# Two store queues, a moved bias add and an earlier transpose in a conditional-residual kernel

## The chip, the cores and the metric

The kernel runs on one core of one Trainium2 chip. The metric is the device time of one launch in microseconds; the span of a profile is the part of it in which the core's engines and queues execute the program.

## What is computed

The input x has 128 batches of 128 tokens and 512 channels. Each batch has a language number, and each of the ten language numbers names a set of weights and rows.

```
w1, w2 = W1[language_ids], W2[language_ids]          # 512x128 and 128x512
h = relu(x @ w1 + b1[language_ids])
y = x + h @ w2 + b2[language_ids]
mean, var = y.mean(-1), ((y - mean) ** 2).mean(-1)
out = x + (y - mean) * rsqrt(var + 1e-5) * gamma[language_ids] + beta[language_ids]
```

All of it is in float32.

## The kernel before, in words

A batch is one tile of 128 partitions (its tokens) by 512 channels. The batches go through a pipeline of stages, and each batch uses all engines:

- TensorE (PE) transposes x in four blocks (`transpose_x`, line 234), multiplies with w1 in four blocks (`down`, line 257) and with w2 (`up`, line 274, two matmul rows in the profile). For a few batches `up` starts with one more matmul that adds b2 into the same accumulator (line 273). Which ones is decided by `b2_by_matmul`.
- ScalarE (ACT) copies the transposed x out of PSUM (line 238), applies b1 and relu (`relu`, line 265), copies w1 of the batch from a resident table (`stage_w1`, line 225) and squares y for the variance (line 310; 394 for the last batches).
- GpSimd (POOL) adds b2 to x (`add_b2`, line 244; not for batches whose b2 comes from a matmul or from VectorE) and beta to x (`add_beta`, line 251). The second sum is the output tile o.
- VectorE (DVE) sums y with its row sums (`residual`, line 291), takes the negative means (line 298), refines the reciprocal root in three small steps (lines 324, 326, 329), scales with gamma (`scale`, line 353) and finishes o (line 362; `finish_cols`, line 419, for the last batches).
- SyncE's queue (SP) issues nearly all transfers. Stores carry two batches each (line 366); the last six batches are stored one by one (`store_last`, line 415).

The order on every engine is written out by hand: `keep` ties each instruction to the one before it on its engine, a DMA to the queue that issues it. A queue waits at an instruction whose inputs are missing, and what stands behind it waits too.

At the start PE runs empty matmuls (`spin`, line 477) while the first loads come. The 30 rows of beta, gamma and b2 are then spread over all partitions: DVE splits the rows into three bfloat16 parts (lines 183 to 187), PE multiplies each with a selecting column (`spread`, line 205) and ACT or DVE copies the result (lines 208 and 210). Between the rows PE does the first batches' transposes (`x_turn`) and down-projections.

At the end `tail` orders the last four batches, 124 to 127, and the ends of 122 and 123 (E is 123). Batches 123 and 124 are finished by ACT and POOL (`by_pool`: line 408 on ACT, 410 and 412 on POOL), 125 half by DVE and half by POOL, 126 and 127 by DVE.

Of the kernel before, what the change touches and what calls it, by code (L numbers as in the profile page):

```python
# [26 lines left out]
def cond_resid_kernel(ctx: ExitStack, tc: tile.TileContext, x, itok, W1, b1, W2, b2, gamma, beta, out):  # L27
# [8 lines left out]
    nc = tc.nc  # L36
    B, S, H = x.shape
# [8 lines left out]
    def keep(ins):  # L46

        engine = ins.ins.engine
        if engine in last:
            tc.add_manual_dep(ins.ins, last[engine], behind, reason="kept order")  # L50
        last[engine] = ins.ins.name
        return ins
# [14 lines left out]
    E = B - 5  # L67
# [6 lines left out]
    def xb(b):  # L74
        return xs[b // G][:, b % G, :]
# [57 lines left out]
    def lid(b, engine):  # L133
        g = b // G
        if (g, engine) not in lids:
            loads, vals = nc.values_load_multi_w_load_instructions(  # L136
                lang[0:1, g * G : (g + 1) * G],
                engines=[engine],
                min_val=0,
                max_val=L - 1,  # L140
                skip_runtime_bounds_check_because="clamped on the chip to 0..L-1 above",
            )
            for ins in loads:
                keep(ins)
            lids[g, engine] = vals
        return lids[g, engine][b % G]
# [65 lines left out]
    xT, hT, rs, os, ys, ssqs, nmeans, rstds = {}, {}, {}, {}, {}, {}, {}, {}  # L212
# [1 line left out]


    def b2_by_matmul(b):
        return b in (0, 1, 2, 3, 5) or (b % 32 == 30 and b < E)

    def b2_by_vector(b):
        return 8 <= b < B - 8 and (b % 4 == 1 if b < 24 else b % 16 in (1, 6, 11))  # L220
# [6 lines left out]
    def transpose_x(b):  # L227
        pxs[b] = p_x.tile([P, KC, P], FP, tag="xT", name=f"pxT_{b}")
        for k in range(KC):
            if b < EARLY:  # L230
                cols = xb(b).rearrange("s (p k) -> s k p", k=KC)[:, k, :]
            else:
                cols = xb(b)[:, k * P : (k + 1) * P]
            keep(nc.tensor.transpose(pxs[b][:, k, :], cols, ident))  # L234

    def copy_xT(b):
        xT[b] = tp.tile([P, KC, P], FP, tag="xT", name=f"xT_{b}")
        keep(nc.scalar.copy(xT[b], pxs.pop(b)))  # L238
# [38 lines left out]
    def col(tiles, b):  # L277

        return tiles[b // 2][:, b % 2 : b % 2 + 1]
# [6 lines left out]
    def residual(b):  # L286
        r = rs.pop(b) if b in rs else xb(b)
        if b % 2 == 0:
            sums[b // 2] = st.tile([P, 2], FP, tag="sum", name=f"sum_{b // 2}")
        keep(  # L290
            nc.vector.scalar_tensor_tensor(ys[b], ys[b], 1.0, r, ALU.mult, ALU.add, accum_out=col(sums, b))  # L291
        )

    def negative_means(g):

        nmeans[g] = st.tile([P, 2], FP, tag="nmean", name=f"nmean_{g}")
        keep(
            nc.vector.scalar_tensor_tensor(  # L298
                nmeans[g], sums[g], -1.0 / H, ys[2 * g + 1][:, 0:2], ALU.mult, ALU.bypass
            )  # L300
        )
# [20 lines left out]
    def newton(n, ssq, t, u):  # L322
        if n == 1:
            keep(nc.vector.scalar_tensor_tensor(u, ssq, EPS * H3, t, ALU.add, ALU.mult))  # L324
        else:
            keep(nc.vector.scalar_tensor_tensor(u, u, 1.0 / H3, t, ALU.mult, ALU.mult))

    def newton_3(rstd, t, u):
        keep(nc.vector.scalar_tensor_tensor(rstd, u, -3.0, t, ALU.add, ALU.mult))
# [11 lines left out]
    def rstd(g, n):  # L341
        t, u = of_pair(g)
        if n < 3:
            newton(n, ssqs[g], t, u)
        else:
            rstds[g] = st.tile([P, 2], FP, tag="rstd", name=f"rstd_{g}")
            newton_3(rstds[g], t, u)
            del ssqs[g], parts_of[g]

    def scale(b):  # L350
        v = lid(b, ET.DVE)
        keep(
            nc.vector.scalar_tensor_tensor(  # L353
                ys[b], ys[b], col(nmeans, b), gamma_b[:, bass.ds(v * H, H)], ALU.add, ALU.mult
            )
        )

    def finish(b):
        g, j = divmod(b, 2)
        o = os[g][:, j, :]  # L360
        keep(
            nc.vector.scalar_tensor_tensor(o, ys.pop(b), rstds[g][:, j : j + 1], o, ALU.mult, ALU.add)  # L362
        )

    def store(g):
        keep(nc.sync.dma_start(out=out[2 * g : 2 * g + 2].rearrange("b s h -> s b h"), in_=os.pop(g)))
        del rstds[g]
# [8 lines left out]
    def of_one(b):  # L376
        if -b not in parts_of:
            pool, tag = {E + 3: (p_h, "h"), E + 4: (p_x, "xT")}.get(b, (p_s, "s"))
            parts_of[-b] = pool.tile([P, 1], FP, tag=tag, name=f"root_of_{b}"), st.tile([P, 1], FP, tag="part", name=f"part_of_{b}")
        return parts_of[-b]  # L380

    def rstd_of(b, n):

        t, u = of_one(b)
        if n < 3:
            newton(n, ssqs[b], t, u)
        else:
            rstds[b] = st.tile([P, 1], FP, tag="rstd", name=f"rstd_{b}")
            newton_3(rstds[b], t, u)

    def deviation_of(b):
        ssqs[b] = st.tile([P, 1], FP, tag="ssq", name=f"ssq_{b}")
        sq = tp.tile([P, H], FP, tag="sq", name=f"sq_{b}")
        keep(nc.scalar.activation(sq, ys[b], AF.Square, bias=col(sums, b), scale=-float(H), accum_out=ssqs[b]))
        root(ssqs[b], of_one(b)[0])

    def rstd_col(b):
        return rstds[b] if b > E else rstds[b // 2][:, b % 2 : b % 2 + 1]
# [5 lines left out]
    def by_pool(b, scaled, cols=slice(0, H)):  # L404

        n = rp.tile([P, H], FP, tag="r", name=f"n_{b}")[:, cols]
        bias = 0.0 if scaled else shifts[b]
        keep(nc.scalar.activation(n, ys[b][:, cols], AF.Identity, bias=bias, scale=rstd_col(b)))
        if not scaled:
            keep(nc.gpsimd.tensor_tensor(n, n, gamma_b[:, bass.ds(lid(b, ET.Pool) * H, H)], ALU.mult))  # L410
        o = os[b // 2][:, b % 2, cols]
        keep(nc.gpsimd.tensor_tensor(o, n, o, ALU.add))  # L412

    def store_last(b):
        keep(nc.sync.dma_start(out=out[b], in_=os[b // 2][:, b % 2, :]))

    def finish_cols(b, cols=slice(0, H)):
        o = os[b // 2][:, b % 2, cols]
# [2 lines left out]
    def tail(b):  # L421
        p = E // 2
        residual(b)
        if b == E + 1:
            rstd(p, 1)
            scale(E - 1)
            rstd(p, 2)
            finish(E - 2)
            store(p - 1)
            rstd(p, 3)  # L430
            deviation_of(b)
            shift(E)
            by_pool(E, False)
        elif b == E + 2:
            rstd_of(b - 1, 1)
            negative_means(b // 2)
            rstd_of(b - 1, 2)
            finish_cols(E - 1)
            store_last(E - 1)
            rstd_of(b - 1, 3)  # L440
            store_last(E)
            deviation_of(b)
        elif b == E + 3:
            left, right = slice(0, H // 2), slice(H // 2, H)
            shift(b - 2)
            by_pool(b - 2, False)
            residual(b + 1)
            store_last(b - 2)
            rstd_of(b - 1, 1)
            scale(b - 1)  # L450
            rstd_of(b - 1, 2)
            negative_means(b // 2)
            deviation_of(b)
            scale(b)
            rstd_of(b - 1, 3)
            rstd_of(b, 1)
            deviation_of(b + 1)
            rstd_of(b, 2)
            finish_cols(b - 1, right)
            by_pool(b - 1, True, left)  # L460
            rstd_of(b, 3)
            scale(b + 1)
            rstd_of(b + 1, 1)
            finish_cols(b)
            store_last(b)
            rstd_of(b + 1, 2)
            store_last(b - 1)
            rstd_of(b + 1, 3)
            finish_cols(b + 1)
            store_last(b + 1)  # L470


    def spin(n, width):
        idle = p_s.tile([P, H], FP, tag="s", name="idle")
        for _ in range(n):
            keep(
                nc.tensor.matmul(
                    idle[:, :width], lhsT=ones, rhs=ones[:, 0:1].to_broadcast([P, width]), start=True, stop=True
                )
            )  # L480


    spin(11, H)

    def spread_turn(lo, hi):
        for r in range(lo, hi):
            spread(r, nc.scalar if r % 7 in (1, 3, 5) else nc.vector)

    def x_turn(b):
        transpose_x(b)  # L490
        copy_xT(b)

    spread_turn(0, 2)
    transpose_x(0)
    transpose_b1()
    copy_xT(0)
    spread_turn(2, 6)
    x_turn(1)
    spread_turn(6, 11)
    down(0)  # L500
    relu(0)
    spread_turn(11, 15)
# [14 lines left out]
    for i in range(3, B + U):  # L517
        b = i - U - 1
# [109 lines left out]
```

## Time and profile before

| | us |
|---|---|
| median of 3 runs (lowest to highest) | 310.78 (310.55 to 310.95) |
| the profiled execution | 310.83 |
| its span | 309.07 |
| last POOL instruction ends | 304.42 |
| last DVE instruction ends | 303.69 |

| engine | busy us | share of the span |
|---|---|---|
| PE | 295.1 | 95% |
| DVE | 294.8 | 95% |
| ACT | 280.4 | 91% |
| POOL | 285.5 | 92% |

Times in the profile count from the span's start. In a timeline a row has the start, the time taken, the engine (with a q for its queue's own instructions, such as issuing a DMA), the line, the operation and out<-in. In a list of waits a row has who waited, for whom, the sum in us, the number of waits and the longest.

### The profile page before, as it was taken

Reading aid. Unit: us, or ns where it says so; the run is one execution under the profiler, and the core shown is the slowest. Engines: PE = TensorE matmul, PEld = TensorE weight load, DVE = VectorE, ACT = ScalarE, POOL = GpSimd, SP = SyncE. Lnnn points to the kernel's source line nnn. Section 1 sums busy time; section 2 is a strip of 40 time slices with the busy share of each in tenths; the row PEclk is TensorE's granted clock in tenths of the full one; section 3 lists DMA queues with packets and bytes.
Section 4 is the critical chain, followed back from the end, with each engine's and each line's share of the span. In section 5 each row is a group of like instructions: output and inputs, shape, how many; then the busy total and the mean of one; then the engine's idle time right before and its main releaser. Section 6 shows DMA issues by size and latency. Waiting matters only on the chain.

```text
span 309.1 us, 6983 instructions
## 1 busy us (share of the span) xinstructions
PE 295.1 (95%) x1842; PEld 220.2 (71%) x1842; DVE 294.8 (95%) x825; ACT 280.4 (91%) x716; POOL 285.5 (92%) x239
## 2 busy tenths in 40 slices
PE   7999999999999999999999999999999999999950
PEld 3758778787777777777777777777777777777720
DVE  6787999999999999999999999999999999999992
ACT  3858999999999999999999999999999999999980
POOL 1349999989999999999999999999999999999993
PEclk9999999999999999999999999999999999999995
DMA  6999979976777666766877565767877666763324
GB/s 235 388 388 387 375 238 362 374 277 232 231 272 271 236 209 220 237 254 214 273 256 271 199 215 223 268 226 252 271 231 259 210 206 252 252 231 137 138 103 170
DMA packets 43481, 77.59 MB, mean 251 GB/s; under 512 B 1929, under 2 KB 7060, under 8 KB 43442
## 3 DMA queue, kind: packets, MB, share of 16 engines
q1 hardware_dynamic: 43382, 77.10, 71.6%
q8 instruction: 15, 0.25, 0.3%
q14 instruction: 24, 0.20, 0.2%
q10 hardware_dynamic: 60, 0.05, 0.1%
HBM read 43.58 MB, written 33.55 MB: 250 GB/s over the span
## 4 chain that ended last, share of the span: by engine, by line
PE 56%; POOL 28%; issue 10%; POOLq 2%; DVE 1%; DMA 1%; ACTq 0%; DVEq 0%
PE ph L257 22%; PE py L274 21%; POOL o L251 17%; PE pxT L234 11%; POOL r L244 9%; PE row L205 2%; POOLq L136 1%; POOL n L410 1%; POOL o L412 1%; POOLq L244 1%; PE py L273 1%; DMA rows<-in_L_cond_b_dram 1%; DVE b_b L210 0%; POOLq L623 0%; DVE left L186 0%
## 5 line engine op out<-in xcount | busy, mean ns | idle before, releaser
L251 POOL TENSOR_TENSOR o<-x,beta_b 128x512 f32<-128x512 f32 x128 | 163.3, 1288 | 9.4 <-DVE beta_b L210 9.4
L257 PE MATMUL ph<-xT,w1s 128*128 128x128 f32 x1024 | 135.4, 275 | 0.0
L244 POOL TENSOR_TENSOR r<-x,b_b 128x512 f32<-128x512 f32 x98 | 126.3, 1288 | 8.8 <-DVE b_b L210 6.2
L274 PE MATMUL py<-w,hT 128*128 x256 | 131.2, 594 | 0.2 <-ACT hT L265 0.2
L257 PEld LDWEIGHTS ph<-xT,w1s 128*128 128x128 f32 x1024 | 124.9, 192 | 1.0 <-ACT hT L265 0.5
L234 PEld LDWEIGHTS pxT<-ident,x 128*128 128x128 f32 x512 | 66.2, 152 | 65.7 <-ACT xT L238 31.9
L353 DVE SCALAR_TENSOR_TENSOR py<-py,nmean,gamma_b 128x512 f32<-128x512 f32 x126 | 95.2, 756 | 0.1
L310 ACT ACTIVATE sq<-py,sum 128x512 f32<-128x512 f32 x124 | 86.3, 696 | 5.7 <-DVE nmean L298 2.9
L362 DVE SCALAR_TENSOR_TENSOR o<-py,rstd,o 128x512 f32<-128x512 f32 x122 | 91.1, 747 | 0.0
L234 PE MATMUL pxT<-ident,x 128*128 128x128 f32 x512 | 78.2, 275 | 0.0
L238 ACT COPY xT<-pxT 128x512 f32<-128x512 f32 x128 | 74.7, 584 | 1.2 <-PE pxT L234 1.2
L291 DVE SCALAR_TENSOR_TENSOR py<-py,r 128x512 f32<-128x512 f32 x98 | 68.0, 694 | 1.5 <-PE py L274 1.1
L225 ACT COPY w1s<-w 128x512 f32 x104 | 64.1, 616 | 0.0
L265 ACT ACTIVATE hT<-ph,b1T 128x128 f32<-128x128 f32 x128 | 47.3, 370 | 4.7 <-PE ph L257 2.5
L274 PEld LDWEIGHTS py<-w,hT 128*128 128x128 f32 x256 | 39.4, 192 | 2.2 <-ACT hT L265 1.1
L310 ACT ACTIVATION_READ_ACCUMULATOR sq<-py,sum 128x1 f32 x124 | 25.4, 205 | 0.0
L291 DVE SCALAR_TENSOR_TENSOR py<-py,x 128x512 f32<-128x512 f32 x30 | 21.0, 698 | 1.6 <-issue 0.9
L320 ACT ACTIVATE root<-ssq,eps 128x2 f32<-128x2 f32 x62 | 16.4, 265 | 2.1
L284 DVE TENSOR_TENSOR py<-py,b_b 128x512 f32<-128x512 f32 x22 | 15.3, 695 | 0.1
L291 DVE DVE_READ_ACCUMULATOR py<-py,r 128x1 f32 x98 | 14.1, 144 | 0.0
L225 ACT COPY w1s<-w1e 128x512 f32 x16 | 9.8, 613 | 1.0 <-DMA w1e<-in_L_cond_W_dram 1.0
L324 DVE SCALAR_TENSOR_TENSOR part<-ssq,root 128x2 f32<-128x2 f32 x62 | 9.5, 153 | 0.9 <-ACT root L320 0.8
(54 smaller groups left out, 95.6 us busy)
## 6 DMA issues: line engine op xcount, KB each, us to landing
out_dram<-o SPq DMA_DIRECT2D x61, 512.0 KB, 3.4
x<-in_x_dram SPq DMA_DIRECT2D x29, 1024.0 KB, 6.7
x<-in_x_dram SPq DMA_DIRECT2D x6, 512.0 KB, 8.9
w1e<-in_L_cond_W_dram SPq DMA_DIRECT2D x2, 1280.0 KB, 11.6
w<-in_L_cond_W_dram SPq DMA_DIRECT2D x4, 640.0 KB, 7.3
w1s<-in_L_cond_W_dram SPq DMA_DIRECT2D x8, 256.0 KB, 8.2
w<-in_L_cond_W_dram SPq DMA_DIRECT2D x1, 1792.0 KB, 10.1
out_dram<-o SPq DMA_DIRECT2D x6, 256.0 KB, 2.0
```

Of the source, the lines that this page charges most:

```text
L225: keep(nc.scalar.copy(w1s[b].rearrange("p k a -> p (k a)"), src))
L234: keep(nc.tensor.transpose(pxs[b][:, k, :], cols, ident))
L238: keep(nc.scalar.copy(xT[b], pxs.pop(b)))
L244: keep(nc.gpsimd.tensor_tensor(rs[b], xb(b), b2_b[:, bass.ds(v * H, H)], ALU.add))
L251: keep(nc.gpsimd.tensor_tensor(os[g][:, j, :], xb(b), beta_b[:, bass.ds(v * H, H)], ALU.add))
L257: nc.tensor.matmul(phs[b], lhsT=w1s[b][:, k, :], rhs=xT[b][:, k, :], start=(k == 0), stop=(k == KC - 1))
L265: keep(nc.scalar.activation(hT[b], phs.pop(b), AF.Relu, bias=b1T[:, bass.ds(lid(b, ET.Activation), 1)]))
L274: keep(nc.tensor.matmul(ys[b], lhsT=hT[b], rhs=w2[:, bass.ds(v * H, H)], start=not m, stop=True))
L291: nc.vector.scalar_tensor_tensor(ys[b], ys[b], 1.0, r, ALU.mult, ALU.add, accum_out=col(sums, b))
L310: nc.scalar.activation(sq, ys[b], AF.Square, bias=col(sums, b), scale=-float(H), accum_out=col(ssqs, b))
L353: nc.vector.scalar_tensor_tensor(ys[b], ys[b], col(nmeans, b), gamma_b[:, bass.ds(v * H, H)], ALU.add, ALU.mult)
L362: nc.vector.scalar_tensor_tensor(o, ys.pop(b), rstds[g][:, j : j + 1], o, ALU.mult, ALU.add)
```

## The change

It does five things:

1. b2 of batch 127 is added by TensorE (`b2_by_matmul`) and no longer by POOL.
2. The stores of 124 and 125 are issued from ACT's queue, after ACT's last instruction; 126 and 127 stay on SP's.
3. In `tail`, DVE's negative means go ahead of the second small step of 125, and the scaling of 127 goes behind the finish of 126.
4. The spin is two matmuls shorter.
5. Batch 0 is transposed and copied before the first table row, b1's transpose follows, and the table rows are dealt out in groups of four and seven instead of two, four and five.

```
     def b2_by_matmul(b):
-        return b in (0, 1, 2, 3, 5) or (b % 32 == 30 and b < E)
+        return b in (0, 1, 2, 3, 5, B - 1) or (b % 32 == 30 and b < E)
...
-    def store_last(b):
-        keep(nc.sync.dma_start(out=out[b], in_=os[b // 2][:, b % 2, :]))
+    def store_last(b, engine=nc.sync):
+        keep(engine.dma_start(out=out[b], in_=os[b // 2][:, b % 2, :]))
...
             residual(b + 1)
-            store_last(b - 2)
             rstd_of(b - 1, 1)
             scale(b - 1)
+            negative_means(b // 2)
             rstd_of(b - 1, 2)
-            negative_means(b // 2)
             deviation_of(b)
...
             by_pool(b - 1, True, left)
+            store_last(b - 2, nc.scalar)
+            store_last(b - 1, nc.scalar)
             rstd_of(b, 3)
-            scale(b + 1)
             rstd_of(b + 1, 1)
             finish_cols(b)
             store_last(b)
             rstd_of(b + 1, 2)
-            store_last(b - 1)
+            scale(b + 1)
             rstd_of(b + 1, 3)
...
-    spin(11, H)
+    spin(9, H)
...
-    spread_turn(0, 2)
-    transpose_x(0)
+    x_turn(0)
     transpose_b1()
-    copy_xT(0)
-    spread_turn(2, 6)
+    spread_turn(0, 4)
     x_turn(1)
-    spread_turn(6, 11)
+    spread_turn(4, 11)
     down(0)
```

## The prediction

> **What bounds the kernel now.** I read the page's head and chain first, then the end of the trace by windows, then the queue that issues the stores, and last the start.
>
> ```profile
> span 309.1 us, 6983 instructions
> ...
> PE 56%; POOL 28%; issue 10%; POOLq 2%; DVE 1%; DMA 1%; ACTq 0%; DVEq 0%
> ```
>
> The chain names PE and then POOL, but it follows engine work and ends with the last POOL add at 304.42. The span ends 4.7 us later. The windows of the end show what fills that time (columns: PE, PEld, DVE, ACT, POOL busy, clock, DMA share, GB/s):
>
> ```profile
> 302.00:303.00 1.00, 0.00 (x0) 0.00 (x0) 0.85 (x4) 0.00 (x0) 0.92 (x2) 0.50 0.68 262
> 303.00:304.00 1.00, 0.00 (x0) 0.00 (x0) 0.69 (x1) 0.00 (x0) 1.00 (x2) 0.50 0.00 0
> 304.00:304.50 0.50, 0.00 (x0) 0.00 (x0) 0.00 (x0) 0.00 (x0) 0.42 (x1) 0.50 0.00 0
> 304.50:305.00 0.50, 0.00 (x0) 0.00 (x0) 0.00 (x0) 0.00 (x0) 0.00 (x0) 0.50 0.76 287
> 305.00:307.00 2.00, 0.00 (x0) 0.00 (x0) 0.00 (x0) 0.00 (x0) 0.00 (x0) 0.50 1.00 382
> 307.00:307.50 0.50, 0.00 (x0) 0.00 (x0) 0.00 (x0) 0.00 (x0) 0.00 (x0) 0.50 0.74 283
> 307.50:309.10 1.60, 0.00 (x0) 0.00 (x0) 0.00 (x0) 0.00 (x0) 0.00 (x0) 0.50 0.00 0
> ```
>
> The transfers stand idle for 1.6 us (303.0 to 304.6), then run full to about 307.4, then 1.7 us pass without data until the span ends. The full stretch is four stores of 256 KB: 4 x 262 KB at 385 GB/s = 2.7 us. Why they start together is in SP's timeline and waits:
>
> ```profile
> 303.77 1.81 SPq L415 DMA_DIRECT2D out_dram<-o  x4
> ...
> SPq L415 <- POOL o L412: 5.8, 2, 3.6
> ```
>
> SP issues in order. Batch 124's store stands ahead of 126, 125 and 127 and waits for POOL's add of 124, which starts at 302.48 and ends about 303.75. The data begins 0.9 us after the first issue (303.77 to about 304.67). What was ready meanwhile is in DVE's timeline:
>
> ```profile
> 301.05 0.15 DVE L329 SCALAR_TENSOR_TENSOR rstd<-part_of,root_of 128x1 f32<-128x1 f32 x1
> 301.11 0.75 DVE L353 SCALAR_TENSOR_TENSOR py<-py,nmean,gamma_b 128x512 f32<-128x512 f32 x1
> 301.77 0.15 DVE L324 SCALAR_TENSOR_TENSOR part_of<-ssq,root_of 128x1 f32<-128x1 f32 x1
> 301.83 0.74 DVE L419 SCALAR_TENSOR_TENSOR o<-py,rstd,o 128x512 f32<-128x512 f32 x1
> 302.49 0.15 DVE L326 SCALAR_TENSOR_TENSOR part_of<-part_of,root_of 128x1 f32<-128x1 f32 x1
> 302.67 0.15 DVE L329 SCALAR_TENSOR_TENSOR rstd<-part_of,root_of 128x1 f32<-128x1 f32 x1
> 302.94 0.75 DVE L419 SCALAR_TENSOR_TENSOR o<-py,rstd,o 128x512 f32<-128x512 f32 x1
> ```
>
> Batch 126 is complete at 302.58 (301.83 + 0.74) and 127 at 303.69. So 126 waited 1.2 us in the queue for nothing of its own.
>
> For the start, the waits between 30 and 34 us and the windows of the first 38 us:
>
> ```profile
> ACT w1s L225 <- DMA w1e<-in_L_cond_W_dram: 1.0, 1, 1.0
> POOL r L244 <- DMA x<-in_x_dram: 0.6, 1, 0.6
> ...
> 8.00:14.00 6.00, 6.00 (x42) 4.48 (x41) 5.30 (x10) 4.78 (x11) 2.50 (x2) 1.00 1.04 385
> 14.00:20.00 6.00, 5.51 (x33) 3.41 (x32) 4.31 (x7) 4.25 (x9) 0.39 (x1) 1.00 1.05 391
> 20.00:26.00 6.00, 6.00 (x32) 4.21 (x31) 4.40 (x14) 3.49 (x9) 6.00 (x6) 1.00 1.05 386
> 26.00:32.00 6.00, 6.00 (x39) 4.62 (x38) 4.99 (x15) 4.55 (x13) 5.97 (x5) 1.00 1.05 387
> ```
>
> The loads run at a full DMA share (1.04 to 1.05) from 8 to 32 us. At 31.2 ACT waits 1.0 us for the table w1e, and at 32.6 POOL waits 0.6 us for x. Both waits are for bytes in a full, fixed queue, so they end when they end, however early the engines come.
>
> **The end, part by part.** POOL: b2 of batch 127 leaves POOL, which is one add of line 244 (293.65 to the next start at 294.88, so 1.23 us). All that follows on POOL moves up by 1.23 if nothing else holds it. Its inputs from ACT are ready: the first two scaled rows end at 296.41 and 298.79, and the half row of 125 (line 408) at 301.70. So 124's add ends at 302.52 instead of 303.75, and 125's left half at 303.19 instead of 304.42.
>
> TensorE: batch 127 gets one more matmul (line 273), 0.38 us by the early rows of the same line, the next matmul starting 0.22 behind it. PE stands idle before the last up-projection, waiting for ACT's hT: the row there is "PE L274 MATMUL py<-w,hT 128*128 x2 [0.23 <-ACT hT L265]", starting at 296.73. In the order of the changed kernel the new matmul waits for an ACT instruction; I take it as the scaling of 123, which ends at 296.41 and is the last reader before relu, so it goes at about 296.45 and the up-projection at 296.7. I take 0. Without that cover it costs 0.22 to 0.6 us (issue distance alone; or busy 0.38 plus the 0.24 that weight loads of line 273 show as issue). A gain is excluded: the up-projection still waits for hT. Behind it stand DVE's sum of 127 (297.96, now from x instead of r, 0.70 either way) and the rest of DVE's end.
>
> DVE: the same instructions in another order. The means go ahead of a small step, so the scaling of 126 (299.64, 0.11 behind what it waited for) starts about 0.07 earlier. The scaling of 127 (0.75) goes behind the finish of 126. The finish of 126 must then wait for its own rstd, which the scaling covered before: by the last two rows above, 302.67 to 302.94, that is 0.27 from rstd's start. So rstd 300.98, finish 301.25 to 301.99; scaling 127 to 302.73; rstd 302.64, finish 302.91 to 303.66. Batch 126 gains 0.59, 127 only 0.03, since its small steps are hidden now but its wait for rstd stays.
>
> Stores: SP keeps 126 and 127; 124 and 125 go to ACT's queue, behind ACT's last work (301.70), so nothing waits behind them. Issues, each about 0.03 after its data: 126 at 302.02 (SP), 124 at 302.55 (ACT), 125 at 303.22 (ACT), 127 at 303.69 (SP). With 0.9 to the first byte the data starts at 302.92, and each later store arrives (303.45, 304.12, 304.59) before the earlier ones are through (303.60, 304.27, 304.95), so the transfers never idle: 302.92 + 2.70 = 305.62. The last store alone would allow 304.59 + 0.68 = 305.27, so bandwidth decides again. With 1.7 us behind it the span is 307.3 instead of 309.07: **1.75 us less**, which is just the distance of the first of the four issues, 303.77 to 302.02.
>
> [...] By the wait row it is 1.75, since the queue was not short of issue time but stood blocked for POOL. [...] I take the row. ACT's queue carried only small rows in this trace, 0.29 to 0.59 per issue against SP's 0.33 to 0.41. The bound is 0 to +0.3 us for the stores of 124 and 125; I take 0, nearest to SP's row.
>
> **The start.** Two spins go, each 0.22 at the granted clock: spinning ends at about 4.6 instead of 5.03. x lands at 4.9 (issue 1.51, 3.4 to landing). Its transposes and b1's (6.34 to 7.06 with their weight load, 0.7) then run from 5.0 to 5.9, while DVE still splits the rows (until 5.86). So the tables' rows start at 5.91 as before, and everything behind the transposes comes up to 0.5 us earlier (DVE's second copy at 6.93 instead of 7.49). I cost it at **nothing** at the end: the waits at 31.2 and 32.6 just grow by 0.5. Bounds: -0.5 (all of it carries) to 0; a slip backwards up to 1.0 is swallowed by the same wait.
>
> **Sum.** The profiled execution took 310.83 for its span of 309.07; less 1.75 that is 309.1. The median of the runs is 310.78, so **309.0**.
>
> **The rivals.**
> - Likeliest (0.65): the end gains 1.75, the start nothing: 309.0, own range 308.7 to 309.4.
> - The start's 0.5 also carries, because the wait at 31.2 is not what paces the middle (0.13): 308.5. Against it: both DMA waits lie behind the start, and DVE and POOL are full afterwards.
> - A new wait eats part of the end (0.13): the extra matmul uncovered (up to 0.6), or ACT's queue late (0.3), each moving the last stores: 309.6. For it: up-projection 127 ends at 297.85 and DVE takes it at 297.96, so no slack lies between.
> - The change doesn't do what it says (0.05): the stores end no earlier because the transfers or the last receipt set the end alone: 310.5. Against it: 1.6 idle us in front of the stores.
> - Slower (0.04): PE's queue runs in order, and the transposes now stand ahead of every table row. If x lands late, all tables start late. The wait at 31.2 swallows 1.0 and the end gives 1.75, so it decides from 2.75 us on, x landing at 7.7 instead of 4.9; with 3.3 us late the time is 311.3. Nothing in the trace suggests such a landing: x is the third issue of SP.
>
> I call 0.2% (0.6 us) the least that a measurement of this kernel tells from no change. Faster than that: 0.65 + 0.13 + 0.13 = 0.91; within 0.05; slower 0.04. The range holds the first three cases but for their far ends: 308.3 to 309.8.
>
> **What would show it.** Right: the first of the last four stores issues near 302.0 and the transfers run without a hole until 305.6; POOL's last add ends near 303.2, DVE's last finish near 303.65; ACT's wait for w1e grows to about 1.5; the middle keeps its times. Wrong: a hole between the stores, line 291 of batch 127 later than 298.0, the w1e wait unchanged with all later times moved, or the tables' rows starting after 6.0.

## The result and the profile after

| | before | changed |
|---|---|---|
| median us (lowest to highest) | 310.8 (310.55 to 310.95, 4 runs) | 308.97 (308.76 to 309.04, 4 runs) |
| ratio, 95% interval | | 0.9941 (0.9923 to 0.9958) |
| profiled execution, its span | 310.83, 309.07 | 308.95, 307.2 |

The change saves 1.8 us. The forecast was 309.0.

The end of the changed kernel, in windows with the same columns as before:

```profile
302.00:303.00 1.00, 0.00 (x0) 0.00 (x0) 0.89 (x3) 0.00 (x0) 1.00 (x2) 0.50 0.30 117
303.00:304.00 1.00, 0.00 (x0) 0.00 (x0) 0.47 (x1) 0.00 (x0) 0.16 (x1) 0.50 0.96 363
304.00:305.00 1.00, 0.00 (x0) 0.00 (x0) 0.00 (x0) 0.00 (x0) 0.00 (x0) 0.50 1.02 385
305.00:305.50 0.50, 0.00 (x0) 0.00 (x0) 0.00 (x0) 0.00 (x0) 0.00 (x0) 0.50 0.94 365
305.50:306.00 0.50, 0.00 (x0) 0.00 (x0) 0.00 (x0) 0.00 (x0) 0.00 (x0) 0.50 0.02 4
306.00:307.20 1.20, 0.00 (x0) 0.00 (x0) 0.00 (x0) 0.00 (x0) 0.00 (x0) 0.50 0.00 0
```

The transfers now run through from 302.7 to 305.5, without the hole that stood at 303.0 to 304.6. The stretch has the same length as before (2.8 us), and 1.7 us without data follow, as before. The four issues behind it, first SP's timeline (126 and 127), then ACT's (124 and 125):

```profile
301.85 1.99 SPq L415 DMA_DIRECT2D out_dram<-o  x2
```
```profile
302.51 1.05 ACTq L415 DMA_DIRECT2D out_dram<-o  x2
```

The first of the four goes at 301.85 instead of 303.77. What it waits for is DVE's finish of 126, the first row below (301.07 + 0.75); the last row is the finish of 127, which ends at 303.47:

```profile
301.07 0.75 DVE L419 SCALAR_TENSOR_TENSOR o<-py,rstd,o 128x512 f32<-128x512 f32 x1
301.74 0.15 DVE L326 SCALAR_TENSOR_TENSOR part_of<-part_of,root_of 128x1 f32<-128x1 f32 x1
301.80 0.75 DVE L353 SCALAR_TENSOR_TENSOR py<-py,nmean,gamma_b 128x512 f32<-128x512 f32 x1
302.46 0.15 DVE L329 SCALAR_TENSOR_TENSOR rstd<-part_of,root_of 128x1 f32<-128x1 f32 x1
302.72 0.75 DVE L419 SCALAR_TENSOR_TENSOR o<-py,rstd,o 128x512 f32<-128x512 f32 x1
```

POOL's last adds (124 and the left half of 125) and TensorE's last matmuls, from their timelines:

```profile
301.21 1.95 POOL L412 TENSOR_TENSOR o<-n,o 128x512 f32<-128x512 f32 x2
```
```profile
296.38 0.38 PE L273 MATMUL py<-parts,pick 96*128 96x512 bf16 x1
296.64 1.12 PE L274 MATMUL py<-w,hT 128*128 x2
```

POOL ends at 303.16, 1.26 earlier. The new matmul of line 273 sits in the gap in which PE waited for hT, and the up-projection starts 0.09 earlier than before (296.73), not later.

The start went another way than forecast. PE's timeline there, before:

```profile
5.91 0.59 PE L205 MATMUL row<-parts,pick 96*128 96x512 bf16 x2 [0.88 <-DVE parts L187]
6.34 0.63 PE L234 MATMUL pxT<-ident,x 128*128 128x128 f32 x4
```

and in the changed kernel:

```profile
4.15 1.06 PE L477 MATMUL idle<-ones 128*128 128x512 bf16 x2
5.10 1.10 PE L234 MATMUL pxT<-ident,x 128*128 128x128 f32 x4
6.13 0.28 PE L193 MATMUL b1p<-ident,b1r 10*128 10x10 f32 x1
6.34 1.27 PE L205 MATMUL row<-parts,pick 96*128 96x512 bf16 x4
```

The four transposes take 1.10 us, against 0.63 for the same four before, and the table rows start at 6.34 instead of 5.91. All nine spins start 0.40 to 0.43 us apart, where the last four of the kernel before are 0.22 apart. So the start gained nothing here: the first scaling of line 353 starts at 23.07, before at 23.04. ACT's wait for w1e is about as long as before (1.0):

```profile
ACT w1s L225 <- DMA w1e<-in_L_cond_W_dram: 1.1, 1, 1.1
```

### The profile page after: what moved, and what is told of

It is laid out like the page before. It is cut to its first block, busy times and chain, and to the rows that moved or that the text cites. A ratio compares the mean times of both kernels' runs of the same rounds, so it can differ in the third digit from the quotient of the medians.

```text
span 307.2 us, 6980 instructions
## 1 busy us (share of the span) xinstructions
PE 296.1 (96%) x1841; PEld 220.6 (72%) x1841; DVE 294.7 (96%) x825; ACT 280.5 (91%) x716; POOL 284.4 (93%) x238
## 5 line engine op out<-in xcount | busy, mean ns | idle before, releaser
L244 POOL TENSOR_TENSOR r<-x,b_b 128x512 f32<-128x512 f32 x97 | 125.0, 1289 | 8.5 <-DVE b_b L210 6.2
L291 DVE SCALAR_TENSOR_TENSOR py<-py,r 128x512 f32<-128x512 f32 x97 | 67.1, 692 | 1.4 <-PE py L274 1.2
```

Source lines behind the costliest of these rows:

```text
L244: keep(nc.gpsimd.tensor_tensor(rs[b], xb(b), b2_b[:, bass.ds(v * H, H)], ALU.add))
```

## The experiments

Three questions were open. Is it the order, the second queue or POOL's shorter work that makes the end earlier? Does the start give or cost anything? And is it really the wait for w1e that hides the start? The theory is that of the prediction: the four stores are bound by their bytes from the first of them on, and the start is swallowed at 31 us. The rivals are that the end needs only one part of the change, and that the start carries through. All runs are against the kernel before on the same chip, whose medians were 310.98, 310.88 and 310.94 us in the three sessions.

**end_only: the changed kernel with the old start.**
```
-    spin(9, H)
+    spin(11, H)
...
-    x_turn(0)
+    spread_turn(0, 2)
+    transpose_x(0)
     transpose_b1()
-    spread_turn(0, 4)
+    copy_xT(0)
+    spread_turn(2, 6)
     x_turn(1)
-    spread_turn(4, 11)
+    spread_turn(6, 11)
```


> The changed kernel with the start of before (11 spins, the first table rows ahead of the transposes). Theory: the whole gain lies behind 297 us, so the time stays at the changed kernel's 309.0 us (within 0.2); the first of the last four stores issues at 301.8 to 302.0. Rival (part of the gain is the start's, the end gives less): 309.3 to 309.5.

Measured: 308.97 us (308.85 to 309.27), ratio 0.9935 (0.9922 to 0.9949). The end alone has the whole gain. In this profile the first of the four stores issued at 302.21, later than expected: this execution was the longest of the five (309.27), and its first scaling started late too, at 23.56.

**start_only: the kernel before with the new start.** The same lines the other way round.

> The kernel before with the start of the changed one alone. Theory: the wait for w1e swallows whatever the start does, 310.8 us (within 0.2), with ACT's wait at 31 us about as long as the start is early or late. Rival (the start carries through): 310.3 if the rows come early, 311.2 if they come 0.4 late as in the changed kernel's profile.

Measured: 310.86 us (310.7 to 311.24), ratio 0.9997 (0.9988 to 1.0006): no difference. In this profile the rows came early; the first scaling of line 353 started at 22.34 instead of 23.04. Its waits around 31 us:

```profile
ACT w1s L225 <- DMA w1e<-in_L_cond_W_dram: 1.8, 1, 1.8
POOL r L244 <- DVE py L291: 1.3, 1, 1.3
```

ACT's wait for w1e has grown from 1.0 to 1.8 and holds all that was won.

**one_queue: all four last stores on SP, in the order 126, 124, 125, 127.**
```
-            store_last(b - 2, nc.scalar)
-            store_last(b - 1, nc.scalar)
...
             store_last(b)
+            store_last(b - 2)
+            store_last(b - 1)
```


> The changed kernel with all four last stores on SP's queue, in the order 126, 124, 125, 127. Theory: the order is what counts, not the second queue, since the data are ready 0.3 to 0.7 us apart and an issue takes 0.33 to 0.41: 309.0 to 309.1 us. Rival (two queues are needed): back by half or more of the gain, 309.8 or later.

Measured: 309.15 us (308.92 to 309.44), ratio 0.994 (0.9926 to 0.9953). A second queue has no gain that shows: 0.2 us by the medians, which is within the interval. From the first of the four issues to the end of the span, the two profiles need the same: 307.7 - 302.39 = 5.3 here, 307.2 - 301.85 = 5.35 in the changed kernel.

**queues_only: the kernel before with 124 and 125 on ACT's queue, nothing else.**

> The kernel before with the stores of 124 and 125 on ACT's queue and nothing else. Theory: 126 goes at 302.6, 127 at 303.7, 124 at 303.8, 125 at 304.5; the data starts at 303.5 but stands idle from 304.2 to 304.6, so it ends at about 306.65 instead of 307.4: 310.1 us. Rival (a second queue saves only issue time): 310.7 to 310.8 us.

Measured: 310.28 us (309.94 to 310.6), ratio 0.9977 (0.9967 to 0.9987). That is 0.6 less than before: taking the blocked stores out of 126's way is a third of the gain. Its first store goes at 302.83 instead of 303.77. That it is the order and not the queue as such which helps is argued here, since 126 only stops waiting for 124; one_queue shows it for the changed kernel.

**b2_on_pool: the changed kernel with b2 of 127 on POOL.**
```
-        return b in (0, 1, 2, 3, 5, B - 1) or (b % 32 == 30 and b < E)
+        return b in (0, 1, 2, 3, 5) or (b % 32 == 30 and b < E)
```


> The changed kernel with b2 of batch 127 added by POOL again. Theory: POOL's two last adds move back by 1.23 us, to about 303.7 and 304.4; the store of 126 still goes at 301.9, the transfers then stand idle from 303.5 to 304.6, and three stores of 0.68 us follow: data until about 306.6, 1.0 us more than the changed kernel, 310.0 us. Rival (the order of the stores alone makes the gain): 309.0 to 309.2.

Measured: 310.03 us (309.62 to 310.28), ratio 0.9969 (0.9958 to 0.9979). The windows of its end show the hole:

```profile
303.00:303.50 0.50, 0.00 (x0) 0.00 (x0) 0.50 (x1) 0.00 (x0) 0.50 (x1) 0.50 1.00 389
303.50:304.00 0.50, 0.00 (x0) 0.00 (x0) 0.15 (x1) 0.00 (x0) 0.50 (x2) 0.50 0.13 45
304.00:304.50 0.50, 0.00 (x0) 0.00 (x0) 0.00 (x0) 0.00 (x0) 0.44 (x1) 0.50 0.00 0
304.50:305.00 0.50, 0.00 (x0) 0.00 (x0) 0.00 (x0) 0.00 (x0) 0.00 (x0) 0.50 0.92 360
```

126 is through by 303.6, and then the transfers stand idle for 0.9 us until 124 and 125 come from POOL. The move of one add from POOL to TensorE is worth about 1 us: 1.06 by the medians, 0.9 by the ratios to the kernel before.

**scale_first: the changed kernel with the scaling of 127 ahead of the finish of 126.**
```
             rstd_of(b, 3)
+            scale(b + 1)
             rstd_of(b + 1, 1)
...
-            scale(b + 1)
```


> The changed kernel with the scaling of 127 back in front of the finish of 126. Theory: 126 ends 0.6 us later (about 302.4), its store is the first of the four, so the transfers start and end 0.5 to 0.6 later: 309.5 us, although the finish of 127 moves by less than 0.1. Rival (the last store, 127, decides): 309.0 us.

Measured: 309.72 us (309.3 to 311.02), ratio 0.9964 (0.9951 to 0.9977). The first of the four issues at 302.40, 0.55 later than in the changed kernel; the finish of 127 ends at 303.49, 0.02 later. So it is the first store, not the last, that sets the end.

**b2_of_126_too: b2 of 126 by TensorE as well** (`B - 2` added to the same list).

> The changed kernel with b2 of batch 126 added by TensorE as well. Theory: POOL loses another add of 1.23 us but then waits for ACT's first scaled row (296.4), so its two last adds end at about 301.5 and 302.2; the store of 124 becomes the first of the four (about 301.6), and the last store, 127 (issue 303.5, first byte 304.4), decides: data until about 305.1 to 305.2 instead of 305.5, so 0.3 to 0.4 us less, 308.6 us. Rival (bandwidth from the first store on is not what decides, or the matmul of 126 delays DVE's sums): 309.0 to 309.4.

Measured: 308.94 us (308.55 to 309.27), ratio 0.9935 (0.9922 to 0.9948). The expected 0.3 to 0.4 didn't show. POOL's last adds do end earlier (301.81 and 302.50) and 124 is now first to be stored, at 301.84, but 126 follows at 302.07 and 127 no earlier than before: its finish ends at 303.69 in this profile. So the expected case didn't come about: DVE's end was 0.22 later in this profile, POOL's adds 0.3 later than expected, and the first store went no earlier than in the changed kernel (301.85). The transfers run from 302.7 to 305.5 as there, and the span is the same 307.2. This fits what scale_first shows, that the first store sets the end. That 127 takes over as the bound isn't shown. Against DVE's end, the first store is some 0.2 us earlier than in the changed kernel, which is less than these runs can tell.

**spin_13 and spin_27: the changed kernel with more empty matmuls at the start**, so that all behind them comes later.
```
-    spin(9, H)
+    spin(13, H)
```


> The changed kernel with 13 spins instead of 9, which moves the first transposes and table rows 0.7 to 1.3 us later (by the moment at which the clock is granted). Theory: the wait for w1e at 31.2 takes it all as long as the rows start before 7.5: 309.0 us (within 0.2) and a wait that is shorter by the shift. Rival (the start carries through): 309.7 to 310.3.

Measured: 309.35 us (308.89 to 309.82), ratio 0.9951 (0.9937 to 0.9965), between what the two theories expected. In the profile batch 0 was 0.37 later than in the changed kernel (the first scaling at 23.44), and batch 12 only 0.07.

> The changed kernel with 27 spins, which makes the first table row start at about 9 to 10.5 (by the moment at which the clock is granted). Theory: the wait for w1e is used up at a row start of about 7.5, what is later than that carries through: 309.0 plus 1.5 to 3.0, 310.5 to 312.0 us, and no wait for w1e. Rival (all of it carries): 309.0 plus 3.2 to 4.2, 312.2 us or later.

Measured: 311.85 us (311.23 to 312.72), ratio 1.0028 (1.0016 to 1.004). The median lies in the theory's range, but the single runs spread over 1.5 us. The profiled execution is the 312.72 one, with the first row at 10.56 and no wait for w1e; by the theory it should have taken 309.0 + 10.56 - 7.5 = 312.1. So it looks as if the wait swallowed less than its length. The table behind the experiments shows how much.

**own_w1_of_8: the changed kernel, batch 8 loads its own w1** instead of copying it from w1e, so that w1e is needed one batch later.
```
-FIRST = 8
+FIRST = 9
...
     load_early(0, 5)
+    load_first(8)
     load_early(5, L)
```


> The changed kernel in which batch 8, too, loads its own w1 (256 KB, between the two halves of w1e), so that batch 9 is the first that needs w1e. Theory: w1e lands 0.7 us later (31.9), but is needed some 2 us later (about 32), so ACT's wait of 1.0 to 1.8 us shrinks to 0 to 0.4 and everything behind it comes 0.8 to 1.2 us earlier: 308.0 us. Rival (that wait doesn't pace the middle, so nothing was swallowed there): 309.0 us, or up to 309.6 since x of batches 10 and 11 lands 0.7 later.

Measured: 308.0 us (307.83 to 308.29), ratio 0.9912 (0.9898 to 0.9925). This beats both kernels (the changed one had the ratio 0.9941 in its own session). In its waits between 28 and 36 us ACT's wait for w1e is gone. POOL's wait for x has become longer instead (line 245 there is line 244 of the other kernels), which costs nothing by the table below:

```profile
POOL r L245 <- DMA x<-in_x_dram: 2.3, 1, 2.3
```

**own_w1_of_8_old_start: the same with the old start.**

> The same with the start of before (11 spins, the first table rows ahead of the transposes). Theory: with the wait gone the start is no longer covered, and the 0.5 us by which the changed start is ahead shows at least in part: 0.3 to 0.5 later than the kernel with the changed start, 308.4 us. Rival (the start is worth nothing anywhere): the same time, 308.0.

Measured: 308.79 us (308.46 to 308.93), ratio 0.9936 (0.9922 to 0.9949): 0.8 later than with the new start by the medians, 0.6 in the spans of the two profiles (306.7 and 306.1), 0.68 at the first scaling. Without the wait the start counts in full, and for somewhat more than the 0.5 that I had given it.

Set beside end_only, these runs say more than each alone. With the new end throughout, the ratios are 0.9935 for neither the new start nor batch 8's own w1, 0.9941 for the new start alone, 0.9936 for the own w1 alone, and 0.9912 for both. Neither edit gains alone; together they gain 0.6 to 0.8 us.

**own_w1_of_8_b2_of_126: both edits together.**

> The kernel with batch 8's own w1, the changed start, and b2 of 126 by TensorE as well. Theory: 0.2 less than without the last, as far as the profile of that edit alone showed: 307.8 us. Rival: no difference, 308.0, since the last store (127) sets the end by then.

Measured: 307.94 us (307.64 to 308.49), ratio 0.9913 (0.9899 to 0.9926): no difference from own_w1_of_8, so b2 of 126 is again worth nothing that shows.

**How much the wait swallows.** The start of a scaling (line 353) for batch 0, ahead of the wait, and for batch 12, behind it, in us, from the timelines of DVE (line 354 where batch 8 has its own w1); the last column is the distance:

| kernel | ACT's wait for w1e | batch 0 | batch 12 | distance |
|---|---|---|---|---|
| own_w1_of_8 | none | 22.34 | 50.80 | 28.46 |
| own_w1_of_8_old_start | none | 23.02 | 51.46 | 28.44 |
| spin_27 | none | 27.04 | 55.49 | 28.45 |
| end_only | 0.4 | 23.56 | 52.02 | 28.46 |
| spin_13 | 0.6 | 23.44 | 51.90 | 28.46 |
| changed | 1.1 | 23.07 | 51.83 | 28.76 |
| before | 1.0 | 23.04 | 51.76 | 28.72 |
| start_only | 1.8 | 22.34 | 51.84 | 29.50 |

The engines need 28.45 us for the distance. Where w1e is in the way, batch 12 doesn't come before 51.8. So the kernel before stood 51.76 - 51.49 = 0.27 behind what its start allowed, not the 1.0 of ACT's wait. In the rows with a loss it is the wait less 0.7 to 0.8 us, and waits of 0.4 and 0.6 lose nothing. By these rows ACT comes to this wait some 0.7 us earlier than what is behind it needs. Batch 8's own w1 also spares ACT one copy, but that isn't what it gains by: spin_27 has that copy and the same distance.

## Why the prediction was right, point by point

- **The end's sum.** Right: forecast 1.75, measured 1.87 in the span, 1.8 in the medians. The first of the four stores issued at 301.85 (forecast 302.02) and the data ended at 305.5 (305.6), 1.7 before the end of the span. DVE's end was 0.2 earlier than worked out. About 0.08 of it was there before the change begins to act (the scaling of batch 118 came 0.08 earlier); the rest arose at line 291 of batch 127 (297.80 instead of 297.96), and I can't say why. Two terms were a little off and nearly cancelled: the data starts 0.8 us behind the first issue, not 0.9, and the four stores take 2.8 us, not 2.7.
- **POOL's add, the extra matmul.** Right: 1.26 forecast as 1.23, and the matmul hidden in PE's wait. b2_on_pool shows that the moved add was needed.
- **The order on DVE.** Right: scale_first loses 0.5 to 0.75, and 127 itself gains next to nothing from it. The earlier negative means (forecast 0.07) had no run of their own.
- **The wait row.** Right: it gave 1.75, and the change brought 1.8. Before, 126 was complete at 302.58 but stood behind the store of 124, which went at 303.77: it had waited behind a blocked store and not for issue time. A second queue as such brings nothing that shows: one_queue is within 0.2 us of the changed kernel (309.15 and 308.97 us, ratios 0.994 and 0.9941).
- **The start: the step "so the tables' rows start at 5.91 as before" failed.** They started at 6.34, one of the prediction's own signs of being wrong. It had each spin at 0.22 and the transposes at the rate of before; the spins stood 0.43 apart, and the four transposes took 1.10 us instead of 0.63. The trace has a record of the granted TensorE clock, which begins when the full clock is granted: at 6.9 us in the changed kernel's profile and at 3.8 in that of before. This is not a matter of the two spins, as the last section shows. In start_only, granted at 4.4, the rows did start at 5.88. With clocks granted at like times the first scaling is earlier by 0.5 to 0.7: 23.04 to 22.34 (before and start_only, granted at 3.8 and 4.4), 23.56 to 23.07 (end_only and changed, 7.2 and 6.9).
- **"I cost it at nothing": right** in the time (end_only and start_only), and for the reason given. But the result itself was no test of it: in its two profiles the gain of the start and the late clock cancelled (23.04 and 23.07), so there was nothing to swallow, and ACT's wait didn't grow to 1.5. That was luck; start_only is the test, with 0.70 earlier at batch 0 and 0.08 later at batch 12. One term was mis-sized: "a slip backwards up to 1.0 is swallowed". The table gives 0.3. The point at which the slower rival decides was therefore 0.3 + 1.75 = 2.05 us and not 2.75. spin_27's profile bears that out: 3.97 later than the changed kernel at batch 0, 3.66 at batch 12.

## What to carry to other kernels

A chain that follows engine work ends with the last engine (here 4.7 us ahead of the span's end, before). Look at the windows behind it: if transfers stand idle and then run at full rate to the end, the first of them counts, and what blocks it in its queue (here 0.55 us at the first store made the time 0.5 to 0.75 longer, in scale_first). Store in the order of readiness; a second queue is one way to get that and was not the point here (one_queue, 0.2 us). And the length of a wait is no measure of what it costs or covers: compare the distance between an event ahead of it and one behind it in two kernels, since an engine that waits may have been early (ACT by some 0.7 us here). An edit that gains nothing may be covered by such a wait: try it again when the wait is gone (the new start gained nothing with the wait for w1e and 0.6 to 0.8 us without it).

## What I had not expected

**When the clock is granted.** Seven kernels have the same instructions on PE in the first 15 us (the changed one, one_queue, b2_on_pool, scale_first, b2_of_126_too, own_w1_of_8 and own_w1_of_8_b2_of_126). In their profiles the record of the full clock begins at 6.9, 6.7, 5.2, 5.2, 5.2, 5.0 and 5.1 us. Over all 12 profiles with 9 or 11 spins it lies between 3.8 and 7.2, with no order by spins, though the first spin starts at 1.19 in each. (The clock column of the windows can't show this: it reads 1.00 where there is no record. The rows do: spins 0.43 us apart ahead of the record and 0.22 in it.) In all 14 profiles the full clock lasts either 293.55 or 296.96 us, which differ by 3.41. What sets the moment, and why there are two lengths, no run shows. With the same start, batch 0 was scaled at 23.00 and 23.07 where the clock came at 6.7 and 6.9, and at 22.34 to 22.58 where it came at 5.0 to 5.2: 0.4 to 0.7 us, which the wait at 31 us swallows in the changed kernel.

**A register load of over 1 us was paid for.** Every four batches PE, ACT, POOL and DVE read language numbers into registers (line 136, 32 loads on each in the profile of before). Around 54 us, where the DMA share is 1.07 in the profile of before, DVE's took, in the profiles of before, changed and one_queue:

```profile
L136 DVEq TENSOR_LOAD <-lang x1: 1200/1200/1200, 54.1 to 54.1; - x1
```
```profile
L136 DVEq TENSOR_LOAD <-lang x1: 406/406/406, 54.2 to 54.2; - x1
```
```profile
L136 DVEq TENSOR_LOAD <-lang x1: 1595/1595/1595, 54.2 to 54.2; - x1
```

The DVE instruction behind it (line 291) came later where the load was long, and all later times moved with it: the scaling of batch 14 is 0.44 later in one_queue than before, 0.12 earlier in the changed kernel, where that of batch 12 agreed within 0.1. Over the 14 profiles, the distance from the scaling of batch 12 to that of 14 is 4.13 or 4.14 us in the eight where this load took 0.35 to 0.94 us. In the other six, with loads of 1.20, 1.20, 1.24, 1.33, 1.36 and 1.60, it is 4.33, 4.33, 4.37, 4.45, 4.49 and 4.72. So here what a load takes beyond 1 us is added in full. That the traffic makes it long is argued, not shown; no run took the traffic away. It may be a part of why runs of one kernel differ by 0.3 to 0.5 us, but each kernel has one profile, so that isn't shown either.
